# Layer 1 of a four-layer graph kernel: a constant in the cubic's real factor, and GpSimd's products merged and asked for earlier

## Chip, cores and metric

One core of one Trainium2 chip. The metric is the device time of one execution in microseconds (us), the median of several runs. In this text PE is TensorE, DVE is VectorE, ACT is ScalarE, POOL is GpSimd and SP is SyncE; PSUM is the matrix engine's accumulator memory and SBUF the on-chip working memory.

## What is computed

Four graph layers over 3327 nodes with 64 features, each `x = layernorm(x + layer(x, adj))`. The change lies in layer 1, whose core is, cut to what matters:

```python
left = x_tan @ att_W[:D] + att_b
right = x_tan @ att_W[D:]
adj_att = sigmoid(left + right.T) * adj            # N x N
x_local = _logmap(x[:, None, :], x[None, :, :], C) # N x N x D
support_t = einsum('ij,ijd->id', adj_att, x_local)
return _proj(_expmap(x, support_t, C), C)
```

The kernel never forms the N x N x D array. For every pair of nodes the scalar weight of `_logmap` is a function of one number, a scaled scalar product of the two rows, and the kernel uses a cubic in it, written as a real linear factor times (a square plus a constant). So per pair (i, j) it needs: a scalar product p, the attention product u = sigmoid(...) * adj, then a = (p + root term) * u, q = (scale * p + shift)^2, v = (q + constant) * a, and a matmul that sums v times the rows of j.

## The kernel before, in words

N is padded to 3328 = 26 blocks of 128. In the hyperbolic layer (`near_sphere`) a block of 128 nodes j lies on the partitions and nodes i lie along the free dimension. The work is 104 tiles of 128 x 832: two halves of i (`cp` 0 and 1), in each half all 26 blocks j, in each block two chunks of 2 x 416 columns. Two tiles with the same block are called a pair here; pair p has tiles 2p and 2p+1.

For each tile t:

- `products(t)`: PE, matmuls of `ljT` and `riT` into a PSUM tile `pq` (3 buffers, L1099).
- `attention(pair)`: the DMA of the block's adjacency rows `at` (4 buffers, L1057; four blocks are resident in `kept`), ACT's sigmoid of 128 x 1664 into `sg` (2 buffers, L1075), and then two POOL products `u = sg * at` of 128 x 832, one for each chunk (4 buffers, L1086).
- `linear(t)`: DVE's `a = (pq + dl) * u` (L1111), then ACT's square of `pq` in place (L1112). `dl` is one value per partition, so a different one for each j.
- `gather(t)`: DVE's `v = (pq + 1.757) * a` (L1120), PE's sum of `v` against the rows `xv` into `acc` (L1132), and `products(t + 3)`.
- `rows_of_sums`: in the first half only, ACT scales one block of `xv` (128 x 63, L1226) for each pair.

The order on PE, ACT, DVE and POOL is written out by hand (`manual_schedule`), so each engine's queue is exactly the order of the calls. In the loop, iteration t calls `linear(t + 1)`, then `gather(t)`, and when t is even `attention(t // 2 + 2)` and `rows_of_sums`. DVE's queue is thus a(1), v(0), a(2), v(1), ...; ACT's is, for each pair, sigmoid, `xv`, square, square.

Before the loop DVE makes `xf`, two columns and the rows `ri` (`rows_of_i`, L1218), POOL makes `dl` and `al` (L1255 to L1257), PE transposes the rows `lf`, `lj` and `ri`, and ACT and DVE copy these out of PSUM (L1210: `rows_j`, `rows_a` and `rows_b` on DVE, the others on ACT). After the loop `near_end` finishes the layer with small operations on 128 x 26 statistics; layers 2 and 3 follow.

Of the kernel before, what the change touches and what calls it, by code (L numbers as in the profile page):

```python
# [19 lines left out]
P = 128  # L20
# [40 lines left out]
CUBIC_ROOT = -1.39229596292  # L61
CUBIC_SHIFT = 0.0453813261445
CUBIC_REST = 1.75705840270866
NEIGH = 100
# [10 lines left out]
def kernel(  # L75
# [819 lines left out]
    with tc.tile_pool(name="l1", bufs=1) as l1:  # L895
# [20 lines left out]
        with tc.tile_pool(name="l1a", bufs=1) as l1a, tc.tile_pool(  # L916
# [86 lines left out]
            vec(ga, vq[:, 1], rq[:, 1], ALU.mult)  # L1003
            stt(inv_s, vq[:, 1], -0.5 / 0.9, r2[:, 1], op0=ALU.mult, op1=ALU.mult)
            sca(aa, g1, -1.0, 1.0, ALU.mult, ALU.add)
            vec(gas, ga, s, ALU.mult)
            stt(lj[:, :, D - 1], aa, 1.0, inv_s, op0=ALU.add, op1=ALU.mult)
        in_order.close()

        def near_sphere(mT, ljT_0, xm, sq_e, t_e, rows_63):  # L1010
# [3 lines left out]
            with tc.tile_pool(name="n1", bufs=1, reuse_waits="tile") as n1, tc.tile_pool(  # L1014
# [50 lines left out]
                def attention(pair):  # L1065

                    if pair >= len(tiles) // 2:
                        return
                    cp, jb, _ = tiles[2 * pair]
                    at, sl = load(cp, jb), slot(jb)  # L1070
                    sg = n1w.tile([P, 2, 2 * CW], F32, tag="sg", name=f"sg_{pair}")
                    lbs = lbh[:, :, cp * 2 * CW : (cp + 1) * 2 * CW]

                    def sigmoid(of):
                        nc.scalar.activation(  # L1075
                            sg[:, :, of], lbs[:, :, of], AF.Sigmoid, bias=rb[:, sl : sl + 1]
                        )

                    chunks = (slice(0, CW), slice(CW, 2 * CW))
                    if pair:  # L1080
                        sigmoid(slice(0, 2 * CW))
                    for ci, of in enumerate(chunks):
                        if not pair:
                            sigmoid(of)
                        u = n1w.tile(TW, F32, tag="u", bufs=4, name=f"u_{pair}_{ci}")
                        nc.gpsimd.tensor_tensor(u, sg[:, :, of], at[:, :, of], ALU.mult)  # L1086
                        us[2 * pair + ci] = u
                        yield
# [16 lines left out]
                def linear(t):  # L1105

                    if t >= len(tiles):
                        return
                    one = slice(slot(tiles[t][1]), slot(tiles[t][1]) + 1)
                    a_s[t] = n1w.tile(TW, F32, tag="a", bufs=3, name=f"a_{t}")  # L1110
                    stt(a_s[t], pqs[t], dl[:, one], us.pop(t), op0=ALU.add, op1=ALU.mult)  # L1111
                    nc.scalar.activation(  # L1112
                        pqs[t], pqs[t], AF.Square, bias=al[:, one], scale=gas[:, one]
                    )
# [109 lines left out]
                def rows_of_sums(jb):  # L1224
                    sl = slot(jb)
                    nc.scalar.activation(  # L1226
                        xv[:, sl, : D - 1], xc[:, sl, : D - 1], AF.Copy, scale=xf[:, sl : sl + 1]
                    )
# [12 lines left out]
                with tc.manual_schedule(  # L1241
# [6 lines left out]
                    keep((NB - 3, NB - 4))  # L1248
                    stt(xf, gas, CUBIC_LEAD / -256.0, gas, op0=ALU.mult, op1=ALU.mult)
                    nc.vector.tensor_copy(ri[:, :, D - 1], ga)  # L1250
                    vec(xv[:, :, D - 1], lj[:, :, D - 1], xf, ALU.mult)
                    rows_of_i(0, 4)
                    rows_of_i(4, NBH)

                    nc.gpsimd.tensor_scalar(dl, g1, CUBIC_ROOT, -1.0, ALU.mult, ALU.add)  # L1255
                    nc.gpsimd.tensor_tensor(dl, dl, inv_s, ALU.mult)
                    nc.gpsimd.tensor_scalar(al, ga, -1.0, CUBIC_SHIFT, ALU.mult, ALU.add)  # L1257
                    spread_a, spread_b = bank(0, left, 0, 4), bank(1, left, 13, 4)
# [6 lines left out]
                    spread_d = alone(left, 17, 3)  # L1265
                    rows_j(copy)
                    spread_c()
                    spread_d()
                    next(start)
                    rows_a = alone(turn, 0, 4)  # L1270
                    rows_a(copy)
                    changed = alone(wrong, 9, 4)
                    changed()
                    rows_b = alone(turn, 4, 4)
                    rows_b(copy)
                    first_ps.close()
                    n1q = pairs.enter_context(
# [9 lines left out]
                    linear(0)  # L1287
                    seventh()
                    for t in range(len(tiles)):
                        linear(t + 1)  # L1290
# [6 lines left out]
                        if t % 2 == 0:  # L1297
                            list(attention(t // 2 + 2))
                            if t // 2 + 2 < NB:
                                rows_of_sums(order[t // 2 + 2])  # L1300
                        if t == 8:
                            spread_left(7)
                        if t == len(tiles) - 4:
# [5 lines left out]
                            gp.tensor_tensor(gk, gs, ga, ALU.mult)  # L1309
                            gp.tensor_tensor(gss, gs, s, ALU.mult)  # L1310
                            gp.tensor_tensor(gks, gk, s, ALU.mult)
                            gp.tensor_scalar(gks, gks, -2.0, None, ALU.mult)
                            gp.tensor_tensor(gs2, gs, gs, ALU.mult)
# [10 lines left out]
                        if t == len(tiles) - 2:  # L1324
# [5 lines left out]
                                t_e.rearrange("p (a k h) -> p a k h", a=2, k=3), pm[..., P:]  # L1330
                            )
                    stt(rxn, r2[:, 0], -0.5, inv_s, op0=ALU.mult, op1=ALU.mult)
                    vec(xn, aa, rxn, ALU.mult)

        def near_end(mT, ljT, xm, sq_e, t_e, rows_63, x2):
# [4 lines left out]
            with tc.tile_pool(name="l1e", bufs=1) as l1e, tc.tile_pool(  # L1340
# [6 lines left out]
                def st(tag):  # L1347
                    return l1e.tile([P, NB], F32, name=f"e_{tag}")
# [70 lines left out]

                gt, q, k, ps = st("gt"), st("q"), st("k"), st("ps")  # L1420
                gp = st("gp")
# [42 lines left out]
                vec(k, p, gks, mul)  # L1464
                vec(gp, p, gss, mul)
                vec(k, k, gt, add)
                vec(ps, p, s, mul)

# [49 lines left out]
                vec(be, be, ck, sub)  # L1518
                alp = of(mul, al, ps, "alp")
                al2 = of(mul, al, al, "al2")  # L1520
# [39 lines left out]
                for b in (3, 1, 2):  # L1560
                    times(mw[b], mT, w_m, *fours[b])
                vec(be, be, s, mul)
                n_r = of(mul, var, t, "n_r")
                vec(n_r, n_r, t, mul)
                stt(n_r, n_r, -3.0, t, op0=add, op1=mul)
                alpha, beta = dl, xf
                stt(alpha, n_r, -0.5, al, op0=mul, op1=mul)
                stt(beta, n_r, -0.5, be, op0=mul, op1=mul)

                for b, g, n in ((0, 0, 1), (0, 1, 3), (3, 12, 1), (1, 4, 4), (2, 8, 4)):  # L1570
# [4 lines left out]
                    vec(lj[:, sl], lj[:, sl], one(beta, sl), mul)  # L1575
                    vec(lj[:, sl], lj[:, sl], pt, add)

                for g, n in threes:
                    sl = slots(g, n)
                    vec(x2[:, sl], x2[:, sl], one(alpha, sl), mul)  # L1580
                    vec(xc[:, sl], xc[:, sl], one(beta, sl), mul)
                    vec(x2[:, sl], x2[:, sl], xc[:, sl], add)
# [270 lines left out]
```

## Time and profile before

| | |
|---|---|
| median of 3 runs | 560.18 us (558.49 to 561.34) |
| the profiled execution | 559.12 us, of which 557.4 us is its span |
| first a (tile 0) starts | 22.22 us |
| last v (tile 103) ends | 226.66 + 1.02 = 227.68 us |
| busy over the span: PE, DVE, ACT, POOL | 525.1, 377.8, 276.2, 215.5 us |

All times in rows are microseconds from the start of the span, unless they are the mean of one instruction, which is in ns. A group's row gives the line of the code, engine and operation, output<-inputs, the shapes and a count, then the busy time and the mean of one, then the idle time of the engine just before these instructions and what ended it. In a timeline row the first number is the start and the second the duration of that row's instructions. Consecutive instructions of one engine overlap a little in these records[...]: DVE starts the instruction after a v 0.93 us later though a v has a duration of 1.02 us. The distance between two starts, not the duration, is what an engine spends on each.

### The profile page before, as it was taken

The page shows a single profiled execution, that of the slowest core. Times are in us where ns is not written, and L with a number is a line of the kernel's source. Part 1 is how long each engine was busy: PE and PEld are TensorE (multiplying, and loading weights), DVE is VectorE, ACT ScalarE, POOL GpSimd, SP SyncE. Part 2 cuts the span into 40 slices and gives each one's busy share as a digit, 9 for nine tenths or more (in the row PEclk, how much of TensorE's full clock was granted, in tenths as well). Part 3 has the DMA queues.
Part 4 walks back from the last instruction along what each step waited for, and adds up shares of the span by engine and source line. Part 5 has one row for each costly group of instructions (what it writes and reads, how often), then busy time and mean ns, then how long its engine had stood idle before and what let it go on. Part 6 is the DMA issues. An engine that isn't in the chain of part 4 may idle for free.

```text
span 557.4 us, 7490 instructions
## 1 busy us (share of the span) xinstructions
PE 525.1 (94%) x2841; PEld 226.5 (41%) x2841; DVE 377.8 (68%) x547; ACT 276.2 (50%) x323; POOL 215.5 (39%) x138
## 2 busy tenths in 40 slices
PE   7889989999999999999999999999999999999991
PEld 5522222222222222764444444444455555545541
DVE  6899999999999999899000010300578877887733
ACT  4799999999999998530000100000364333433321
POOL 3699999999999999300000000000001000000000
PEclk9899999999999999899999999999999999999996
DMA  8977776766676717799999039999019994799601
GB/s 287 357 254 232 209 229 201 224 210 227 206 237 211 220 60 272 294 427 425 422 423 418 16 141 422 420 426 413 15 55 328 342 327 177 244 270 362 257 1 37
DMA packets 33893, 143.57 MB, mean 258 GB/s; under 512 B 10269, under 2 KB 11959, under 8 KB 28855
## 3 DMA queue, kind: packets, MB, share of 16 engines
q1 hardware_dynamic: 31511, 142.40, 69.9%
q10 hardware_dynamic: 2336, 0.59, 0.5%
q8 instruction: 24, 0.39, 0.3%
q14 instruction: 22, 0.18, 0.1%
HBM read 141.53 MB, written 0.87 MB: 255 GB/s over the span
## 4 chain that ended last, share of the span: by engine, by line
PE 66%; DVE 20%; ACT 8%; issue 3%; DMA 1%; DVEq 0%
PE cnt L419 25%; PE pq L1099 12%; DVE v L1120 12%; PE cnt L524 11%; PE acc L720 6%; ACT sg L1075 4%; PE acc L735 3%; ACT pq L1112 3%; DVE a L1111 2%; DVE w L537 1%; PE cnt L410 1%; DVE mask L339 1%; DMA x<-in_x 1%; PE x_w L1435 1%; PE pn_l L371 1%
## 5 line engine op out<-in xcount | busy, mean ns | idle before, releaser
L1086 POOL TENSOR_TENSOR u<-sg,at 128x832 f32<-128x832 f32 x88 | 169.9, 1959 | 3.5 <-ACT sg L1075 3.1
L1099 PE MATMUL pq<-riT,ljT 64*128 64x416 f32 x416 | 100.2, 560 | 15.2 <-DVE v L1120 6.2
L1111 DVE SCALAR_TENSOR_TENSOR a<-pq,dl,u 128x832 f32<-128x832 f32 x104 | 112.1, 1078 | 2.9 <-PE pq L1099 2.8
L1112 ACT ACTIVATE pq<-pq,al,gas 128x832 f32<-128x832 f32 x104 | 105.0, 1011 | 15.2 <-DVE a L1111 14.3
L1120 DVE SCALAR_TENSOR_TENSOR v<-pq,a 128x832 f32<-128x832 f32 x104 | 105.8, 1017 | 1.1 <-ACT pq L1112 0.7
L1132 PE MATMUL acc<-v,xv 128*64 128x416 f32 x416 | 95.4, 537 | 0.1
L1075 ACT ACTIVATE sg<-lb,rb 128x1664 f32<-128x1664 f32 (+1 forms) x53 | 87.3, 1647 | 0.1
L539 ACT ACTIVATE w<-cnt 128x832 int16<-128x832 f32 x55 | 47.2, 863 | 71.5 <-PE cnt L524 71.4
L419 PE MATMUL cnt<-at_l,lj 128*64 128x416 f32 x448 | 80.2, 513 | 0.0
L651 POOL TENSOR_TENSOR s<-sq,s 128x384 bf16<-128x384 f32 (+1 forms) x4 | 4.1, 1026 | 195.0 <-ACT s L650 195.0
L504 ACT ACTIVATE x<-cnt 128x416 f32<-128x416 f32 x8 | 4.1, 517 | 130.6 <-PE cnt L419 130.6
L1099 PEld LDWEIGHTS pq<-riT,ljT 64*128 64x128 f32 x416 | 31.5, 184 | 88.3 <-DVE v L1120 83.0
L537 DVE TENSOR_SCALAR w<-cnt 128x832 int16<-128x832 f32 x49 | 50.2, 1024 | 25.2 <-PE cnt L524 23.8
L524 PE MATMUL cnt<-mask,tri 128*128 128x416 bf16 x208 | 53.5, 339 | 0.1
L720 PE MATMUL acc<-w,s 128*128 128x416 bf16 x208 | 52.6, 339 | 0.5 <-DVE hid L792 0.5
L524 PE MATMUL cnt<-mask,rest 128*128 128x416 bf16 x200 | 51.6, 340 | 1.2 <-ACT w L539 0.6
L419 PEld LDWEIGHTS cnt<-at_l,lj 128*64 128x64 f32 x448 | 31.9, 137 | 46.0 <-issue 45.2
L1132 PEld LDWEIGHTS acc<-v,xv 128*64 128x64 f32 x416 | 20.6, 134 | 61.0 <-issue 57.8
L339 DVE TENSOR_SCALAR mask<-ah 128x1664 bf16<-128x1664 f32 x42 | 43.4, 1034 | 0.5 <-DMA ah<-in_adjT 0.5
L407 DVE COPY lj<-pn_l 128x512 f32<-128x512 f32 (+1 forms) x4 | 2.4, 592 | 60.9 <-PE pn_l L371 60.9
L419 PE MATMUL cnt<-kept,lj 128*64 128x416 f32 x224 | 41.2, 513 | 0.0
L1086 POOL TENSOR_TENSOR u<-sg,kept 128x832 f32<-128x832 f32 x16 | 31.0, 1959 | 3.6 <-ACT sg L1075 3.6
(286 smaller groups left out, 411.7 us busy)
## 6 DMA issues: line engine op xcount, KB each, us to landing
at_l<-in_adjT SPq DMA_DIRECT2D x24, 1664.0 KB, 13.2
at<-in_adjT SPq DMA_DIRECT2D x44, 832.0 KB, 5.0
ah<-in_adjT SPq DMA_DIRECT2D x42, 832.0 KB, 6.5
bt_l<-in_adjT SPq DMA_DIRECT2D x8, 1664.0 KB, 16.8
kept<-in_adjT SPq DMA_DIRECT2D x7, 1664.0 KB, 9.2
lb<-lf_rows SPq DMA_DIRECT2D x2, 384.0 KB, 4.3
ljT<-ljT SPq DMA_DIRECT2D x4, 128.0 KB, 5.2
x<-in_x ACTq DMA_DIRECT2D x1, 416.0 KB, 5.3
```

Source lines behind the costliest of these rows:

```text
L339: nc.vector.tensor_scalar(mask[q], at, 0.0, None, ALU.not_equal)
L419: nc.tensor.matmul(acc[c][h * D : (h + 1) * D, :], hw[:, slot(jb), :], blocks[jb][:, o : o + CW], start=c not in begun, stop=last, skip_gr ...
L524: nc.tensor.matmul(cnt[c][:, e, :], mat, mask[q][:, of], start=start, stop=(mat is tri), skip_group_check=True,)
L537: nc.vector.tensor_scalar(w.bitcast(I16), cnt[c], 0.0, None, ALU.max)
L720: nc.tensor.matmul(acc[h, c][:, e, :], s12[:, slot(jb)].rearrange("p t d -> p (t d)"), ws[q, c][:, e, :], start=first, stop=last,)
L1075: nc.scalar.activation(sg[:, :, of], lbs[:, :, of], AF.Sigmoid, bias=rb[:, sl : sl + 1])
L1086: nc.gpsimd.tensor_tensor(u, sg[:, :, of], at[:, :, of], ALU.mult)
L1099: nc.tensor.matmul(pq[:, h, :], ljT[h != jb // NBH][rows, of], riT[rows, ch * CW : (ch + 1) * CW], start=True, stop=True,)
L1111: stt(a_s[t], pqs[t], dl[:, one], us.pop(t), op0=ALU.add, op1=ALU.mult)
L1112: nc.scalar.activation(pqs[t], pqs[t], AF.Square, bias=al[:, one], scale=gas[:, one])
L1120: stt(w, pqs.pop(t), CUBIC_REST, a_s.pop(t), op0=ALU.add, op1=ALU.mult)
L1132: nc.tensor.matmul(accs[cp, ci][h * D : (h + 1) * D, :], xv[:, slot(jb), :], w[:, h, :], start=(jb == orders[cp][0]), stop=(jb == orders[c ...
```

## The change

Five things.

1. The rows `lj` are scaled by `s` on DVE (`scaled`, three pieces) and the last columns hold other values, so that the linear factor's shift is the same for all j: a is now `(pq + CUBIC_PLUS) * u`, with a constant in place of the per-partition `dl`. The square takes `ga` in place of `gas`, `xv` is scaled by a new `gss = xf * s`, and a few small multiplications by `s` disappear or move in `near_end`.
2. The product is written over the sigmoid's tile: `u` disappears and `sg` gets 4 buffers.
3. From pair 2 on POOL makes both chunks of a pair in one instruction of 128 x 1664.
4. `attention` is called one pair further ahead (`t // 2 + 3`), with `attention(2)` before the loop.
5. POOL's first product stands behind a one-column copy, `after`, of the last piece that DVE scales; `rows_j` and `rows_a` are copied by ACT, and the second half of the first sigmoid is asked for after them.

```diff
+CUBIC_PLUS = 2 * CUBIC_ROOT - 1
...
-            stt(inv_s, vq[:, 1], -0.5 / 0.9, r2[:, 1], op0=ALU.mult, op1=ALU.mult)
...
-            stt(lj[:, :, D - 1], aa, 1.0, inv_s, op0=ALU.add, op1=ALU.mult)
+            sca(lj[:, :, D - 1], aa, 1.0, None, ALU.add)
...
-                    sg = n1w.tile([P, 2, 2 * CW], F32, tag="sg", name=f"sg_{pair}")
+                    sg = n1w.tile([P, 2, 2 * CW], F32, tag="sg", bufs=4, name=f"sg_{pair}")
...
-                    for ci, of in enumerate(chunks):
+                    wide = slice(0, 2 * CW)
+                    for of in chunks if pair < 2 else (wide,):
                         if not pair:
                             sigmoid(of)
-                        u = n1w.tile(TW, F32, tag="u", bufs=4, name=f"u_{pair}_{ci}")
-                        nc.gpsimd.tensor_tensor(u, sg[:, :, of], at[:, :, of], ALU.mult)
-                        us[2 * pair + ci] = u
+                        nc.gpsimd.tensor_tensor(sg[:, :, of], sg[:, :, of], at[:, :, of], ALU.mult)
+                        for ci, c in enumerate(chunks):
+                            if of in (c, wide):
+                                us[2 * pair + ci] = sg[:, :, c]
...
-                    stt(a_s[t], pqs[t], dl[:, one], us.pop(t), op0=ALU.add, op1=ALU.mult)
+                    stt(a_s[t], pqs[t], CUBIC_PLUS, us.pop(t), op0=ALU.add, op1=ALU.mult)
                     nc.scalar.activation(
-                        pqs[t], pqs[t], AF.Square, bias=al[:, one], scale=gas[:, one]
+                        pqs[t], pqs[t], AF.Square, bias=al[:, one], scale=ga[:, one]
                     )
...
-                    stt(xf, gas, CUBIC_LEAD / -256.0, gas, op0=ALU.mult, op1=ALU.mult)
-                    nc.vector.tensor_copy(ri[:, :, D - 1], ga)
+                    def scaled(b, n):
+
+                        sl = slice(2 * b, 2 * (b + n))
+                        vec(
+                            lj[:, sl, : D - 1], lj[:, sl, : D - 1],
+                            s[:, sl].unsqueeze(2).to_broadcast([P, 2 * n, D - 1]), ALU.mult,
+                        )
+
+                    scaled(9, 4)
+                    sca(ri[:, :, D - 1], ga, -CUBIC_ROOT, None, ALU.add)
+                    rows_of_i(0, 4)
+                    stt(xf, ga, CUBIC_LEAD / -256.0, ga, op0=ALU.mult, op1=ALU.mult)
                     vec(xv[:, :, D - 1], lj[:, :, D - 1], xf, ALU.mult)
-                    rows_of_i(0, 4)
-                    rows_of_i(4, NBH)
-
-                    nc.gpsimd.tensor_scalar(dl, g1, CUBIC_ROOT, -1.0, ALU.mult, ALU.add)
-                    nc.gpsimd.tensor_tensor(dl, dl, inv_s, ALU.mult)
-                    nc.gpsimd.tensor_scalar(al, ga, -1.0, CUBIC_SHIFT, ALU.mult, ALU.add)
+                    vec(gss, xf, s, ALU.mult)
+                    rows_of_i(4, 8)
+                    scaled(5, 4)
+                    rows_of_i(8, NBH)
+                    scaled(0, 5)
+
+                    nc.gpsimd.tensor_scalar(
+                        al, ga, CUBIC_PLUS, CUBIC_SHIFT - CUBIC_ROOT, ALU.mult, ALU.add
+                    )
+
+                    after = n1.tile([P, 1], F32, name="after")
+                    nc.gpsimd.tensor_copy(after, lj[:, 0, :1])
...
-                    rows_j(copy)
                     spread_c()
                     spread_d()
-                    next(start)
+                    rows_j()
                     rows_a = alone(turn, 0, 4)
-                    rows_a(copy)
+                    rows_a()
                     changed = alone(wrong, 9, 4)
                     changed()
                     rows_b = alone(turn, 4, 4)
                     rows_b(copy)
+                    next(start)
...
                     seventh()
+                    list(attention(2))
                     for t in range(len(tiles)):
...
-                            list(attention(t // 2 + 2))
+                            list(attention(t // 2 + 3))
...
-                vec(ps, p, s, mul)
...
-                vec(be, be, s, mul)
...
+                vec(beta_c, beta, s, mul)
```

More of the change, by code (lines that the diff above doesn't have):

```diff
@@ L1226, in rows_of_sums @@
                     nc.scalar.activation(
-                        xv[:, sl, : D - 1], xc[:, sl, : D - 1], AF.Copy, scale=xf[:, sl : sl + 1]
+                        xv[:, sl, : D - 1], xc[:, sl, : D - 1], AF.Copy, scale=gss[:, sl : sl + 1]
                     )
@@ L1309, in near_sphere @@
                             gp.tensor_tensor(gk, gs, ga, ALU.mult)
-                            gp.tensor_tensor(gss, gs, s, ALU.mult)
-                            gp.tensor_tensor(gks, gk, s, ALU.mult)
-                            gp.tensor_scalar(gks, gks, -2.0, None, ALU.mult)
+                            gp.tensor_scalar(gks, gk, -2.0, None, ALU.mult)
                             gp.tensor_tensor(gs2, gs, gs, ALU.mult)
@@ L1331, in near_sphere @@
                             )
+                    stt(inv_s, vq[:, 1], -0.5 / 0.9, r2[:, 1], op0=ALU.mult, op1=ALU.mult)
                     stt(rxn, r2[:, 0], -0.5, inv_s, op0=ALU.mult, op1=ALU.mult)
@@ L1418, in p_of @@
                         )
-                gt, q, k, ps = st("gt"), st("q"), st("k"), st("ps")
+                gt, q, k = st("gt"), st("q"), st("k")
                 gp = st("gp")
@@ L1464, in near_end @@
                 vec(k, p, gks, mul)
-                vec(gp, p, gss, mul)
+                vec(gp, p, gs, mul)
                 vec(k, k, gt, add)
-                vec(ps, p, s, mul)
                 first = in_bank("first_w")
@@ L1518, in near_end @@
                 vec(be, be, ck, sub)
-                alp = of(mul, al, ps, "alp")
+                alp = of(mul, al, p, "alp")
                 al2 = of(mul, al, al, "al2")
@@ L1565, in near_end @@
                 stt(n_r, n_r, -3.0, t, op0=add, op1=mul)
-                alpha, beta = dl, xf
+                alpha, beta, beta_c = dl, xf, gss
                 stt(alpha, n_r, -0.5, al, op0=mul, op1=mul)
@@ L1580, in near_end @@
                     vec(x2[:, sl], x2[:, sl], one(alpha, sl), mul)
-                    vec(xc[:, sl], xc[:, sl], one(beta, sl), mul)
+                    vec(xc[:, sl], xc[:, sl], one(beta_c, sl), mul)
                     vec(x2[:, sl], x2[:, sl], xc[:, sl], add)
```

## The prediction, made before the changed kernel was run

> **What bounds the kernel now.** I read the page first, then the timeline of layer 1, then the waits. The chain of waits gives layer 1's loop (a at 22.22 us to the last v's end at 227.68 us) to three engines in turn: v on DVE, pq on PE, the sigmoid on ACT. That is a loop with several nearly equal engines, so their distances between starts matter and not their shares. The groups on the page:
>
> ```profile
> L1086 POOL TENSOR_TENSOR u<-sg,at 128x832 f32<-128x832 f32 x88 | 169.9, 1959 | 3.5 <-ACT sg L1075 3.1
> L1111 DVE SCALAR_TENSOR_TENSOR a<-pq,dl,u 128x832 f32<-128x832 f32 x104 | 112.1, 1078 | 2.9 <-PE pq L1099 2.8
> L1112 ACT ACTIVATE pq<-pq,al,gas 128x832 f32<-128x832 f32 x104 | 105.0, 1011 | 15.2 <-DVE a L1111 14.3
> L1120 DVE SCALAR_TENSOR_TENSOR v<-pq,a 128x832 f32<-128x832 f32 x104 | 105.8, 1017 | 1.1 <-ACT pq L1112 0.7
> ```
>
> a and v have one shape, one PSUM input, one SBUF input and the same pair of operations; they differ in the scalar, a column of `dl` in a and a constant in v. The column costs 61 ns an instruction. DVE waits 4 us in all and POOL hardly: both are full. Which sets the pace? POOL's rows of the timeline:
>
> ```profile
> 84.79 46.55 POOL L1086 TENSOR_TENSOR u<-sg,at 128x832 f32<-128x832 f32 x24 [1.01 <-ACT sg L1075]
> 131.74 77.26 POOL L1086 TENSOR_TENSOR u<-sg,at 128x832 f32<-128x832 f32 x40 [0.41 <-ACT sg L1075]
> ```
>
> In the second half POOL runs 40 products without a gap at 77.26/40 = 1.93 us, 3.863 us a pair. DVE alone would need 0.99 (start of a to start of v) + 0.93 (v to a) = 1.92, 3.85 a pair. From tile 56 (a at 133.72) to tile 102 (222.57) the loop takes 88.85/23 = 3.863 us a pair: POOL's pace. In the first half it is 3.88 us (tile 36 at 94.59 to tile 48 at 117.88, 23.29/6), and the timeline tells why:
>
> ```profile
> 103.98 0.33 ACT L1226 ACTIVATE xv<-xc,xf 128x63 f32<-128x63 f32 x1
> 104.22 1.00 ACT L1112 ACTIVATE pq<-pq,al,gas 128x832 f32<-128x832 f32 x1
> 104.27 1.08 DVE L1111 SCALAR_TENSOR_TENSOR a<-pq,dl,u 128x832 f32<-128x832 f32 x1
> ...
> 105.26 1.02 DVE L1120 SCALAR_TENSOR_TENSOR v<-pq,a 128x832 f32<-128x832 f32 x1
> ...
> 105.38 1.02 ACT L1112 ACTIVATE pq<-pq,al,gas 128x832 f32<-128x832 f32 x1 [0.16 <-DVE a L1111]
> 106.20 1.08 DVE L1111 SCALAR_TENSOR_TENSOR a<-pq,dl,u 128x832 f32<-128x832 f32 x1
> 106.33 1.67 ACT L1075 ACTIVATE sg<-lb,rb 128x1664 f32<-128x1664 f32 x1
> ...
> 107.90 0.33 ACT L1226 ACTIVATE xv<-xc,xf 128x63 f32<-128x63 f32 x1
> 108.14 2.11 ACT L1112 ACTIVATE pq<-pq,al,gas 128x832 f32<-128x832 f32 x2
> ...
> 109.17 1.02 DVE L1120 SCALAR_TENSOR_TENSOR v<-pq,a 128x832 f32<-128x832 f32 x1
> ```
>
> A square waits for its a (105.35 -> 105.38); behind it stand sigmoid, `xv` and the next square, which ends at 109.14, and only then v starts (109.17, not 109.11). From the square's start to that v is 3.79 us. That is a ring through ACT and DVE, and it is longest in the first half, since only there `xv` (0.24 us) is in it.
>
> **Part by part.**
>
> *A constant in a.* a should cost what v costs: 0.93 us from start to start instead of 0.99, so DVE needs 4 x 0.9325 = 3.73 us a pair. Second half: 3.863 -> 3.73 if POOL lets it, 26 x 0.13 = 3.5 us. First half: I solve the ring. Let x be the distance from a(t+1) to v(t), T the pair's period. DVE: T = x + 3 intervals. ACT: T + x = a's duration + 0.03 + 3.79. Before: T = x + 2.85 and T + x = 4.90, so T = 3.875 (3.88 measured: the ring is right). After: T = x + 2.80 and T + x = 4.84, so T = 3.82. So the first half gains 0.06 a pair, not 0.12: from pair 3 on, 23 x 0.06 = 1.4 us.
>
> *Products of both chunks at once.* No 128x1664 row exists on POOL. From rows: 128x832 takes 1.957 us, and a small product
>
> ```profile
> L1309 POOL TENSOR_TENSOR gk<-gs,ga 128x26 f32<-128x26 f32 x1 | 0.2, 239 | 0.1
> ```
>
> gives a slope of (1957-239)/806 = 2.13 ns, so 239 + 1638 x 2.13 = 3.73 us, some 3.70 from start to start: just under DVE's 3.73. The dearest end is that nothing is saved, 2 x 1.93 = 3.86; the cheapest is the slope alone, 1664 x 2.13 = 3.55. I take 3.70, the fit through both rows. [...] Writing over the input is at no cost: the in-place `dl` product of 128x26 (L1256) takes 242 ns beside 239.
>
> [...] The row: all 104 a lie between 1073 and 1085 ns with POOL at work all the time. [...] I add nothing.
>
> *A pair further ahead, four `sg`.* Steadily at no cost: a sigmoid then waits for an a of four pairs earlier. At the start it costs, since ACT must make one more sigmoid (1.57 us) before the loop settles. SP's order is unchanged apart from that; an `at` still waits for POOL four pairs earlier, with 5.0 us to landing against over 11 us of cover.
>
> *The start.* DVE's work before the loop grows from 15.81 to 18.20 us by three scalings of 504, 504 and 630 columns[...] (the distance between starts of 128x512 products in `near_end` is 0.60 us): 0.60 + 0.60 + 0.73, and 0.1 each for some small ones; it ends near 20.2 us. POOL's first product starts then at about 20.4 us instead of 18.50. From there: four single products, 20.4 + 4 x 1.93 = 28.1; pair 2's merged product ends at 31.9 us, so a(4) starts at 31.9 instead of 29.86 (+2.0). ACT on its side takes over two copies (0.5 us each) and the extra sigmoid, 2.6 us, against 0.5 us that it now idles: +2.1 us. Before: a(6) at 33.70. After: ACT reaches the square of tile 4 near 34.1, v(4) at 35.1, a(6) at 36.0 (+2.3). I take +2.2. PE is not late: its transposes wait for `lj` and `ri` pieces that DVE has done before PE comes to them (16.4 and 18.0 us). `rows_b` stays on DVE at 21.0 us, and the first pq at 21.1.
>
> *Small operations.* In `near_end` the product with `s` at 233.67 us leaves a chain of dependent work: -0.1. The one at 240.38 stood in a wait for a reciprocal: nothing. `beta_c` comes after `lj` is done, beside PE's next layer. `inv_s` moves to 227.6 us, into a wait of DVE of 0.79 us for PE; if that cover went it would cost 0.1. Two POOL products fewer at 227 us are off the path. Two PE stalls of DVE (1.17 us before tile 16, 1.14 before tile 28) stay: they are v(14) and v(26), a pq and then a, whatever DVE's pace.
>
> *What is late next.* In the second half DVE itself, with POOL 0.03 us a pair behind it; PE needs 0.97 + 0.92 us a tile by durations, 1.8 from start to start. Layer 2 starts from the layer's end: its transfers wait for the last `acc` matmuls, so the gain is passed on whole.
>
> Sum against the profiled execution: 559.1 + 2.2 - 1.4 - 3.5 - 0.1 = **556.3 us**. The profiled execution lies 1.1 us below the median, so against the median this is 557.4. A measurement of this kernel can tell about 0.5%, 2.8 us, from no change; the forecast gain is just that.
>
> **The rivals.**
> *ACT does not hold the first half* (0.25): if a's earlier ends and sigmoids no longer tied to POOL let the ring run at DVE's 3.73 us, the first half gains another 23 x 0.09 = 2.1 us and part of the start is made up: 553.8. For it: ACT waits 14.3 us for a now, idle time that an engine at its limit would not have. Against it: the solved ring gives the measured 3.88.
> *The constant saves nothing* (0.08): if a's 61 ns came from reading `u` beside POOL's writing, DVE stays at 3.85 and the loop pays the start and gets 26 x 0.01 back: 561. Against it: v reads a tile just like u.
> *Slower: the merged product is dear* (0.07). POOL sets the end: 28.1 + 50 x P + 4.7 (last product to last v). That is 227.7, today's end, at P = 3.9 us; at 4.0 it is 232.8, 564 us. For it: no row of this size. Against it: two separate ones take 3.86, and only a long or in-place instruction with a price of its own would exceed that.
> *The start is dearer* (0.2): the scalings meet POOL's work on `rest` at 16.1 us and each other's waits, +3.5 us instead of 2.2: 557.6.
> Base case 0.40.
>
> **How the numbers follow.** Faster by over 0.5% (under 556.3 from the profiled time, 557.4 from the median): the ACT rival, and half or more of the base: 0.55. Same: the rest of the base, the dear start, most of the constant rival: 0.38. Slower: the merged product and a little of the constant rival: 0.07. Range 553.2 to 560.0: from below the ACT rival to the dear start with the median's 1.1 us on top; beyond it lie the slow product and the useless constant.
>
> **What would show it.** a's group at 1017 ns; 50 POOL rows of 128x1664 at 3.73 us; POOL's first product at 20.4 us; a(4) near 31.9 and a(6) near 36.0; 3.82 us a pair in the first half with v waiting for ACT, 3.73 in the second; the last v's end near 225. It would be wrong if a stayed at 1078, if the merged product exceeded 3.8 us, or if DVE showed waits for POOL in the second half.

## The result, and the profile after

| | before | after |
|---|---|---|
| median, us (11 runs each, side by side) | 559.12 | 557.58 |
| lowest and highest | 558.37 to 561.34 | 556.09 to 559.05 |
| ratio, 95% interval | | 0.9964 [0.9949, 0.9979] |
| the profiled execution, and its span | 559.12, 557.4 | 557.54, 555.7 |
| first a starts | 22.22 | 22.20 |
| a(6) starts | 33.70 | 35.34 |
| last v ends | 227.68 | 224.34 |
| a pair, first half (a 36 to a 48) | 3.882 | 3.823 |
| a pair, second half (a 56 to a 102) | 3.863 | 3.725 |
| last v's end to layer 2's first matmul | 15.33 | 16.78 |

The kernel is 0.36% faster, 1.5 us. The same groups of the page after the change; a row gives busy time and the mean of one in ns, then the idle time before:

```profile
L1088 POOL TENSOR_TENSOR sg<-sg,at 128x1664 f32<-128x1664 f32 x44 | 163.7, 3738 | 3.7 <-ACT sg L1076 2.2
...
L1116 ACT ACTIVATE pq<-pq,al,ga 128x832 f32<-128x832 f32 x104 | 104.6, 1012 | 12.1 <-DVE a L1115 12.0
L1115 DVE SCALAR_TENSOR_TENSOR a<-pq,sg 128x832 f32<-128x832 f32 x104 | 105.3, 1013 | 4.5 <-PE pq L1103 2.3
L1124 DVE SCALAR_TENSOR_TENSOR v<-pq,a 128x832 f32<-128x832 f32 x104 | 105.4, 1014 | 3.3 <-ACT pq L1116 2.2
```

a now costs what v costs, 1013 ns beside 1014. v's listed waits for ACT have grown from 0.7 to 2.2 us, most of it at the start: v(1) and v(2) wait 0.33 and 1.15 us there, before 0 and 0.59. Inside the first half, where DVE has become quick enough to find the square late, v's waits (tiles 8 to 51) sum to 1.1 us instead of 0.1, most of them too short to be listed. POOL's rows of the timeline (start, duration):

```profile
20.06 0.19 POOL L1277 COPY after<-lj 128x1 f32<-128x1 f32 x1 [4.48 <-DVE lj L1256]
20.21 15.06 POOL L1088 TENSOR_TENSOR sg<-sg,kept 128x832 f32<-128x832 f32 x6
...
100.96 7.46 POOL L1088 TENSOR_TENSOR sg<-sg,at 128x1664 f32<-128x1664 f32 x2 [0.19 <-ACT sg L1076]
...
131.88 70.75 POOL L1088 TENSOR_TENSOR sg<-sg,at 128x1664 f32<-128x1664 f32 x19 [0.52 <-ACT sg L1076]
```

POOL starts later than before (20.21 instead of 18.50 us), pauses every second pair in the first half for ACT's sigmoid, and runs 19 merged products in the second half at 70.75/19 = 3.724 us. The ring of the first half, ACT's and DVE's rows:

```profile
104.86 1.01 DVE L1115 SCALAR_TENSOR_TENSOR a<-pq,sg 128x832 f32<-128x832 f32 x1
...
109.70 1.02 DVE L1124 SCALAR_TENSOR_TENSOR v<-pq,a 128x832 f32<-128x832 f32 x1
```

```profile
105.91 1.02 ACT L1116 ACTIVATE pq<-pq,al,ga 128x832 f32<-128x832 f32 x1 [0.16 <-DVE a L1115]
106.86 1.67 ACT L1076 ACTIVATE sg<-lb,rb 128x1664 f32<-128x1664 f32 x1
108.43 0.33 ACT L1230 ACTIVATE xv<-xc,gss 128x63 f32<-128x63 f32 x1
108.67 1.99 ACT L1116 ACTIVATE pq<-pq,al,ga 128x832 f32<-128x832 f32 x2
```

From the square at 105.91 to the v (109.70) that waits for the square behind sigmoid and `xv` it is 3.79 us as before, and from a to that v 4.84 us: the two numbers that the prediction's ring gave.

**Where the time went.** Stretch by stretch, the profiled executions differ by +1.64 us up to a(6), by -4.98 us from there to the last v's end (193.98 before, 189.00 after), by +1.45 us from there to layer 2, and by +0.19 us after that: -1.70 us of span. The +1.45 is not in the loop, and the diff's edits in that stretch only take out or move small multiplications. In the stretch from 229.2 to 236.2 us (columns: length, then busy time of PE, its weight load, DVE, ACT and POOL, the granted clock of PE, DMA) the first execution of this kernel has

```profile
229.20:236.20 7.00, 7.00 (x35) 7.00 (x35) 4.80 (x39) 4.72 (x13) 0.00 (x0) 0.52 0.99 421
```

about half the clock: PE is always busy but has 35 matmuls there. A second profiled execution of the same kernel (below) has 48 there, at clock 1.00, in 5.50 us of work.

### The profile page after: what moved, and what is told of

It reads as the page before. It is cut to its first block, busy times and chain, and to the rows that moved or that the text cites. A ratio compares the mean times of both kernels' runs of the same rounds, so it can differ in the third digit from the quotient of the medians.

```text
span 555.7 us, 7392 instructions
## 1 busy us (share of the span) xinstructions
PE 527.5 (95%) x2841; PEld 226.9 (41%) x2841; DVE 372.2 (67%) x549; ACT 276.8 (50%) x325; POOL 207.4 (37%) x85
## 4 chain that ended last, share of the span: by engine, by line
PE 68%; DVE 17%; issue 7%; ACT 6%; POOL 1%; DVEq 0%; POOLq 0%; ACTq 0%
PE cnt L421 26%; PE cnt L526 11%; DVE v L1124 10%; PE pq L1103 9%; PE acc L722 6%; PE acc L1136 4%; PE acc L737 3%; ACT pq L1116 3%; ACT sg L1076 2%; DVE a L1115 2%; DVE w L539 1%; PE cnt L412 1%; DVE mask L341 1%; PE idle L928 1%; PE x_w L1455 1%
## 5 line engine op out<-in xcount | busy, mean ns | idle before, releaser
L1088 POOL TENSOR_TENSOR sg<-sg,at 128x1664 f32<-128x1664 f32 x44 | 163.7, 3738 | 3.7 <-ACT sg L1076 2.2
L1116 ACT ACTIVATE pq<-pq,al,ga 128x832 f32<-128x832 f32 x104 | 104.6, 1012 | 12.1 <-DVE a L1115 12.0
L1115 DVE SCALAR_TENSOR_TENSOR a<-pq,sg 128x832 f32<-128x832 f32 x104 | 105.3, 1013 | 4.5 <-PE pq L1103 2.3
L421 PEld LDWEIGHTS cnt<-at_l,lj 128*64 128x64 f32 x448 | 31.9, 137 | 46.2 <-issue 45.4
L586 DVE TENSOR_TENSOR x<-x,xc 128x416 f32<-128x416 f32 x4 | 2.4, 588 | 41.5 <-ACT x L506 41.5
```

What stands on the lines that cost most here:

```text
L421: nc.tensor.matmul(acc[c][h * D : (h + 1) * D, :], hw[:, slot(jb), :], blocks[jb][:, o : o + CW], start=c not in begun, stop=last, skip_gr ...
L1088: nc.gpsimd.tensor_tensor(sg[:, :, of], sg[:, :, of], at[:, :, of], ALU.mult)
L1115: stt(a_s[t], pqs[t], CUBIC_PLUS, us.pop(t), op0=ALU.add, op1=ALU.mult)
L1116: nc.scalar.activation(pqs[t], pqs[t], AF.Square, bias=al[:, one], scale=ga[:, one])
```

## The experiments

Periods of a pair in the loop's two halves, starts of a(6) and ends of the last v, and ratios to the kernel before with their intervals:

| kernel | first half, second half | a(6), last v ends | ratio |
|---|---|---|---|
| before | 3.882, 3.863 | 33.70, 227.68 | |
| after | 3.823, 3.725 | 35.34, 224.34 | 0.9964 [0.9949, 0.9979] |
| column given back | 3.882, 3.846 | 35.49, 228.83 | 1.0039 [1.0023, 1.0056] |
| two products again | 3.820, 3.725 | 37.37, 226.26 | 0.9946 [0.9927, 0.9965] |
| before, constant only | 3.840, 3.838 | 32.47, 224.72 | 0.9958 [0.9947, 0.9969] |
| before, sigmoid a square earlier | 3.845, 3.847 | 34.39, 226.78 | 0.9988 [0.9979, 0.9998] |
| no gate | 3.822, 3.725 | 35.26, 224.28 | 0.9963 [0.9951, 0.9975] |
| xv behind the next square | 3.725, 3.725 | 35.49, 222.27 | 0.9919 [0.9899, 0.9938] |
| the same, no gate | 3.725, 3.725 | 35.18, 221.98 | 0.9925 [0.9905, 0.9946] |
| xv behind, two products | 3.725, 3.765 | 35.14, 222.92 | 0.9955 [0.9942, 0.9968] |
| xv behind, sigmoids later | 3.725, 3.725 | 35.69, 222.48 | 0.9913 [0.9889, 0.9936] |
| the same, no gate | 3.725, 3.725 | 37.22, 224.02 | 0.9937 [0.9913, 0.9962] |
| two pairs ahead | 4.68 in the second half | | one execution: 599.95 us |

**The changed kernel again, a second profiled execution.** No edit.

> The changed kernel once more, unedited, for a second look at the granted clock after the loop. If the 6.8 us at half clock there (229.2 to 235.9 us) is a matter of when a spell falls and not of the change: another length or none, and from the last v's end to the next layer's first matmul about 15.35 us instead of 16.78. If the change itself brings it about: 6.8 us and 16.8 again.

The loop is the same to 0.01 us a pair (3.822 and 3.725, last v's end 224.29). From there to layer 2 it takes 15.37 us instead of 16.78, and the execution 555.96 us instead of 557.54:

```profile
229.20:236.20 7.00, 5.50 (x48) 5.30 (x48) 5.37 (x43) 5.08 (x14) 0.00 (x0) 1.00 1.01 426
```

So the 1.4 us behind the loop belong to the execution and not to the change. Spells at half the clock, 3.4 or 6.8 us long, stand in each of the twelve traces for which the clock was taken in steps of 0.5 us, besides one at the end of the span in before and after, in whose last 11.1 us PE is idle (mean clock 0.57 and 0.59): before has one from 12.0 to 18.9 us and one from 233.9 to 237.3, after has 14.1 to 17.5, 27.8 to 31.2 and 229.2 to 236.0. The ten of them that cover the end of layer 1 bear the reading out: from the last v's end to layer 2 it takes 15.33 to 15.38 us in the five that have no spell there, 15.33 to 15.71 in the four with one of 3.4 us, and 16.78 in the one with 6.8 us.

In the 3.4 us ahead of the spell of 6.8 us PE is recorded as busy throughout (3.40 of 3.40 us from 225.8 to 229.2), at clock 1.00 up to 229.0; what brings this spell about is not shown.

Of the other ten timed runs of the kernel only the mean clock is known. Of all eleven, the two at 0.987, the second execution's clock, took 556.1 and 556.3 us, and the nine at 0.979 to 0.983 took 557.3 to 559.1. That fits one spell more in most runs than in the second execution; where it fell is not known, and the kernel before shows no such plain order.

**The column given back.** What the constant is worth, all else as changed:

```diff
-                    stt(a_s[t], pqs[t], CUBIC_PLUS, us.pop(t), op0=ALU.add, op1=ALU.mult)
+                    stt(a_s[t], pqs[t], plus, us.pop(t), op0=ALU.add, op1=ALU.mult)
```

`plus` is a 128 x 1 tile that POOL fills with CUBIC_PLUS.

> The changed kernel with one edit: a takes the same number from a one-column tile instead of an instruction constant. If the constant is what shortens a: a's mean goes back from 1013 to about 1077 ns, the second half runs at DVE's 3.85 us a pair instead of 3.72 (26 x 0.13 = 3.3 us) and the first half at the ring's 3.875 instead of 3.82 (23 x 0.055 = 1.3 us); the last v ends near 229.0 instead of 224.3 us and the time is about 4.6 us above the changed kernel's, near 562. If the gain came from GpSimd's merged and earlier products alone: no change, 557.6.

```profile
L1115 DVE SCALAR_TENSOR_TENSOR a<-pq,plus,sg 128x832 f32<-128x832 f32 x104 | 111.6, 1073 | 4.4 <-PE pq L1103 2.3
```

The same value, once read from a column and once a constant, makes 1073 or 1013 ns: the 60 ns are the column's. The second half then takes 3.846 us a pair, twice 0.99 + 0.93: DVE's own pace with a column, and not the 3.863 of before. The last v ends 4.5 us later than in the changed kernel, and the time is above the kernel before.

**Two products again**, with the rest of the change (lead, four `sg`, constant):

```diff
-                    for of in chunks if pair < 2 else (wide,):
+                    for of in chunks:
```

> The changed kernel with two products of 128x832 for each pair, in place, instead of one of 128x1664. If the merged product is what frees the second half (as the prediction had it, 3.863 us a pair on POOL against 3.73): the second half goes back to 3.863 and the last v ends near 227.8, time near 561. If what mattered is that POOL no longer waits for sigmoids (four buffers, a pair further ahead): POOL runs without a gap from 20.2 us, 104 x 1.93 = 200.9, so it ends at 221.1 and the last v near 224.3, because its lead of some 3 us at half time is just used up at the end; time near 557.7, with a(4) some 1.5 us earlier than with the merged product.

```profile
36.89 49.94 POOL L1088 TENSOR_TENSOR sg<-sg,at 128x832 f32<-128x832 f32 x26
87.61 119.16 POOL L1088 TENSOR_TENSOR sg<-sg,at 128x832 f32<-128x832 f32 x62 [0.79 <-DVE v L1124]
```

The second half stays at 3.725 us although POOL needs 2 x 119.16/62 = 3.84 us a pair. POOL hardly stops, in the first half too, where DVE needs 3.82 and loses another 2.3 us at two stalls for PE; with a longer lead it has by then a stock of products that it uses up. At a(56) the product is ready 3.8 us ahead of its a, at a(100) still 1.2 us. That a(6) stands at 37.37 goes with a spell of half clock from 15.1 to 22.0 us ahead of it, in which PE's transposes are late (first a at 23.71); the edit changes nothing ahead of a(4). The whole loop (first a to last v's end) takes 202.55 us instead of 202.14, but the difference lies ahead of a(6): from there it is 188.89 us instead of 189.00. So in the changed kernel the merged product buys nothing in the settled loop, and not the 3.5 us that the second half gained; in the times, 0.9946 and 0.9964, the two do not stand apart either.

**The kernel before with the constant alone.** All j get the same linear factor, another one than the layer needs; the instructions are those of the kernel before.

```diff
-                    stt(a_s[t], pqs[t], dl[:, one], us.pop(t), op0=ALU.add, op1=ALU.mult)
+                    stt(a_s[t], pqs[t], CUBIC_ROOT, us.pop(t), op0=ALU.add, op1=ALU.mult)
```

> The kernel before with one edit: a takes a constant instead of its column (the linear factor is then another one than the layer needs). If the loop is bound by POOL and by ACT's ring as read: a falls to 1014 ns, yet the second half stays at 3.863 us a pair and the first half goes from 3.88 to 3.86 at best, so the last v ends at 226.9 to 227.7 and the time is within 1 us of before's. If DVE alone were the bound: 104 x 0.06 = 6.3 us less, the last v near 221.4.

```profile
129.41 76.79 POOL L1086 TENSOR_TENSOR u<-sg,at 128x832 f32<-128x832 f32 x40 [0.39 <-ACT sg L1075]
```

The second half does not stay at 3.863 but falls to 3.838, and POOL makes 40 products in 76.79 instead of 77.26 us, with nothing changed on POOL. Either the column slows POOL's products, or 3.863 was never POOL's pace. The rows of the kernel before show what else it can be, DVE's, ACT's and POOL's in turn:

```profile
151.11 1.08 DVE L1111 SCALAR_TENSOR_TENSOR a<-pq,dl,u 128x832 f32<-128x832 f32 x1
...
156.90 1.08 DVE L1111 SCALAR_TENSOR_TENSOR a<-pq,dl,u 128x832 f32<-128x832 f32 x1
```

```profile
152.22 1.02 ACT L1112 ACTIVATE pq<-pq,al,gas 128x832 f32<-128x832 f32 x1 [0.35 <-DVE a L1111]
153.16 1.67 ACT L1075 ACTIVATE sg<-lb,rb 128x1664 f32<-128x1664 f32 x1
```

```profile
154.91 1.96 POOL L1086 TENSOR_TENSOR u<-sg,at 128x832 f32<-128x832 f32 x1
```

a(t+1) ends at 152.19, its square starts at 152.22, the sigmoid behind it at 153.16, the product at 154.91, and a(t+4) when that ends: 5.79 us, and 1.93 more to a(t+5), where the next round begins. That is 7.72 us for two pairs, 3.86 each: a second ring, of four steps on three engines (a on DVE, square and sigmoid on ACT, product on POOL). In it POOL has only gaps of some hundredths of a microsecond, too small for the profile to call them waits: over pairs 30 to 49 its starts lie 1.91 us apart inside a pair, and 1.95 us from one pair to the next.

**The kernel before with the sigmoid a square earlier** tells the two apart, with the column kept:

```diff
+                    list(attention(2))
                     for t in range(len(tiles)):
...
                         if t % 2 == 0:
-                            list(attention(t // 2 + 2))
                             if t // 2 + 2 < NB:
                                 rows_of_sums(order[t // 2 + 2])
+                        else:
+                            list(attention((t + 1) // 2 + 2))
```

> The kernel before (column, single products, two sg), with nothing changed but the call of attention: for each pair it stands one tile earlier, so ACT's sigmoid comes ahead of the second square of a pair instead of behind it. In the kernel before, the second half's rows close a ring: a (151.11 us) - its square (152.22) - the sigmoid (153.16) - POOL's product (154.91) - the a three tiles later (156.90), 5.79 us for three tiles, 3.86 a pair. Theory A, that ring set the second half's 3.863: with the sigmoid a square earlier it falls to DVE's own 3.846 (as in the kernel with the column given back), POOL's free pace of 2 x 1.92 = 3.84 being just below; first half also to about 3.85, since sigmoid and xv no longer stand together; second half's 46 tiles 0.4 us shorter. Theory B, POOL's own pace set it, because the column read slows its product: the second half stays at 3.863 with POOL without a gap at 1.93. The start may cost up to 2 us, since a sigmoid more stands ahead of the loop; time within 0.5% of the kernel before by both.

```profile
129.50 76.85 POOL L1086 TENSOR_TENSOR u<-sg,at 128x832 f32<-128x832 f32 x40 [0.38 <-ACT sg L1075]
```

Both halves fall to 3.846 us, DVE's pace with a column, and POOL makes 40 products in 76.85 us beside a DVE that reads the column. POOL's starts now lie 1.91 us apart inside a pair and 1.92 to the next. So the ring set the second half, and POOL's own pace is 1.92 us, 3.84 a pair. What this kernel gains in the loop it pays in part at the start (a(6) 34.39 instead of 33.70).

**xv behind the next square.** If ACT's ring holds the first half, taking `xv` out of it must bring DVE's pace there:

```diff
                             list(attention(t // 2 + 3))
-                            if t // 2 + 2 < NB:
-                                rows_of_sums(order[t // 2 + 2])
+                        elif t // 2 + 2 < NB:
+                            rows_of_sums(order[t // 2 + 2])
```

> The changed kernel with ACT's scaling of a block of xv asked for after odd tiles instead of after even ones, so that it stands behind the next square and not ahead of it. If ACT's ring (square, sigmoid, xv, square, v) sets the first half: the ring loses 0.24 us, falls below DVE's 3.72 us a pair, the first half goes from 3.82 to 3.73 (23 x 0.09 = 2.1 us), no v waits for a square there, and the last v ends near 222.2; time near 555.5. If ACT's sum of work set it (3.7 us a pair of issue) or POOL did: 3.82 stays and 557.6.

```profile
103.02 1.01 ACT L1116 ACTIVATE pq<-pq,al,ga 128x832 f32<-128x832 f32 x1
103.95 0.34 ACT L1230 ACTIVATE xv<-xc,gss 128x63 f32<-128x63 f32 x1
104.23 1.02 ACT L1116 ACTIVATE pq<-pq,al,ga 128x832 f32<-128x832 f32 x1
105.18 1.67 ACT L1076 ACTIVATE sg<-lb,rb 128x1664 f32<-128x1664 f32 x1
106.75 1.01 ACT L1116 ACTIVATE pq<-pq,al,ga 128x832 f32<-128x832 f32 x1
```

It does: 3.725 us in both halves. `xv` now fills a wait of the square for its a (the next square starts 0.28 us after it, where it had to wait anyway), and between the square at 104.23 and the next at 106.75 only the sigmoid stands. The last v ends 2.1 us earlier than in the changed kernel; with 554.61 us, a ratio of 0.9919, the kernel is faster than both.

**The same with two products.** With POOL's stock no longer refilled in a slower first half, the merged product should count:

```diff
-                    for of in chunks if pair < 2 else (wide,):
+                    for of in chunks:
```

> xv asked for after odd tiles, and two products of 128x832 for each pair. With the ring short, DVE could run at 3.725 us a pair throughout; two products take POOL 2 x 1.92 = 3.84. If the merged product is worth something only when ACT's ring no longer hides POOL: 104 x 1.92 = 199.7 us from POOL's first product near 20.3 puts its end at 220.0 and the last v near 223.2, 1 us later than with the merged product (222.3) but with no 3.725 kept up in the second half; time near 555.5. If the merged product is worth its 0.115 us a pair over all 50 pairs: 5.8 us, time near 560.

```profile
210.09 3.93 POOL L1088 TENSOR_TENSOR sg<-sg,kept 128x832 f32<-128x832 f32 x2
```

```profile
210.22 1.02 DVE L1115 SCALAR_TENSOR_TENSOR a<-pq,sg 128x832 f32<-128x832 f32 x1
...
214.05 1.02 DVE L1115 SCALAR_TENSOR_TENSOR a<-pq,sg 128x832 f32<-128x832 f32 x1
```

It does, but only near the end. POOL makes 88 products in 168.80 us without a stop, 3.84 a pair, and DVE at 3.725 catches up with it by 0.1 us a pair: the product is ready 2.0 us ahead of a(40), 0.35 ahead of a(80), and from a(86) on each pair's first a starts as its product ends (214.02 and 214.05 in the rows), 3.83 us a pair. The average of the second half is 3.765. From a(6) to the last v's end it takes 187.78 us instead of 186.79 with merged products, so there the merged product is worth 1.0 us; it gives 0.35 of that back at the start, where a(6) comes later with it (35.49 instead of 35.14).

**No gate.** The copy `after` and its tile are left out, so POOL's first product needs only its sigmoid.

> The changed kernel without the one-column copy that holds POOL's first product back until DVE has scaled its last piece. My theory: the gate is most of what the new start costs. POOL then begins near 17.5 us, its second product near 21.2 (it waits for ACT), pair 2's merged product ends near 30.7 instead of 31.6 us, and a(4) follows[...]. Loop from a(0) to the last v's end shorter by some 0.8 us or a(0) earlier; time 0.5 to 1 us below the changed kernel's. Rival: [...] a(0) and a(4) are later than with the gate: time 1 to 2 us above.

DVE's rows ahead of the loop:

```profile
17.90 2.46 DVE L1256 TENSOR_TENSOR lj<-lj,s 128x504 f32<-128x504 f32 x1
20.28 0.80 DVE L1222 SCALAR_TENSOR_TENSOR mT<-xc,gas 128x630 f32<-128x630 f32 x1
```

POOL's first product starts at 17.59 us, and the scaling that DVE asks for next takes 2.46 us instead of 0.68: it ends at 17.90 + 2.46 = 20.36 us, 0.54 us after POOL's product (17.59 + 2.23 = 19.82). Beside that product, this one piece with two SBUF inputs cost 1.78 us more. Against the expectation a(4) does not come at 30.7 but at 31.54 us (31.61 with the gate), and a(6) is 35.26 instead of 35.34: the gate neither costs nor saves, since v(1) and v(2) wait for ACT's squares in both (0.88 and 1.16 us without it). Together with `xv` behind the next square it changes nothing either (last v's end 221.98 instead of 222.27, times 554.88 and 554.61):

> xv asked for after odd tiles and no gate, together. If both hold by themselves, they add, because with a short ring DVE follows POOL from the start: 3.73 us a pair throughout, last v near 221.4 us, time 0.5 to 1 us below that with xv alone (554.6). If the gate is needed, above it.

**Sigmoids later at the start.** On the kernel with `xv` behind the next square, ACT's sigmoids of pairs 2 and 3 go behind the squares of tiles 1 and 2:

```diff
-                    list(attention(2))
                     for t in range(len(tiles)):
                         linear(t + 1)
                         if t == 0:
                             by_rows()
                             rows_of_sums(order[1])
+                            list(attention(2))
+                        if t == 1:
+                            list(attention(3))
...
                         if t % 2 == 0:
-                            list(attention(t // 2 + 3))
+                            if t:
+                                list(attention(t // 2 + 3))
```

> The changed kernel with xv behind the next square, and with ACT's sigmoids of pairs 2 and 3 asked for one square later each (behind the squares of tiles 1 and 2 instead of ahead of them). Theory A, ACT alone holds the start: v(1) and v(2) no longer wait for squares, a(4) starts near 30.7 us instead of 31.6, a(6) near 34.5 and the last v ends near 221.4 us. Theory B, POOL holds it just as much, since its first product stands behind the gate at 20.2 us: four single products and a merged one end at 20.2 + 4 x 1.93 + 3.70 = 31.6 us, so a(4) stays at 31.6, a(6) at 35.3, the last v's end at 222.2 us and the time at 0.992 of the kernel before. I expect B.

```profile
29.05 1.02 DVE L1124 SCALAR_TENSOR_TENSOR v<-pq,a 128x832 f32<-128x832 f32 x1 [0.21 <-ACT pq L1116]
31.96 1.02 DVE L1115 SCALAR_TENSOR_TENSOR a<-pq,sg 128x832 f32<-128x832 f32 x1 [1.88 <-POOL sg L1088]
```

In the changed kernel these two read

```profile
30.48 1.02 DVE L1124 SCALAR_TENSOR_TENSOR v<-pq,a 128x832 f32<-128x832 f32 x1 [1.15 <-ACT pq L1116]
31.61 1.02 DVE L1115 SCALAR_TENSOR_TENSOR a<-pq,sg 128x832 f32<-128x832 f32 x1
```

The wait for ACT is nearly gone, and a(4) waits for POOL instead and starts no earlier. Both engines were due at the same time: ACT with its extra sigmoid, and POOL, which started at 20.21 us and finished its first merged product near 31.6.

**And without the gate as well**, the one kernel in which the start should gain:

> As the kernel with later sigmoids, and POOL's first product is not held behind DVE's last scaling either. If ACT and POOL hold the start together, only this one gains: POOL's second product starts near 21.4 us (as without the gate before), so pair 2 ends at 21.4 + 3 x 1.93 + 3.70 = 30.9 us: a(4) 30.9 instead of 31.6, last v's end 221.5 us, time 0.991. If the gate or the sigmoids alone hold it, this is either at 222.2 like the others (something third holds it), or no better than the one with later sigmoids alone.

```profile
17.65 1.92 DVE L1266 TENSOR_TENSOR gss<-xf,s 128x26 f32<-128x26 f32 x1
```

It did not, but for a reason beside the question: a small product of 128 x 26, 0.18 us elsewhere, now took 1.92 us and ended at 19.57 us, 0.04 us after POOL's first product (17.54 + 1.99 = 19.53), PE's transposes were late (first a at 23.73) with a spell of half clock from 15.2 to 22.0 us, as in the kernel with two products, and POOL's second product started at 23.53 us instead of 21.4, when its sigmoid was there. Whether the start gains when both holds are gone is not settled.

**The changed kernel with attention two pairs ahead**, as in the kernel before:

```diff
-                    list(attention(2))
...
-                            list(attention(t // 2 + 3))
+                            list(attention(t // 2 + 2))
```

> The changed kernel with attention asked for two pairs ahead as in the kernel before, all else left (merged products, constant, gate). Theory A, the merged product needs the longer lead: the sigmoid of pair p+2 is asked for at v(2p), and a(2p+4) then waits for sigmoid 1.6 + square ahead of it 1.0 + merged product 3.7 us = 6.3 us or more, while DVE's four instructions until that a take only some 2.8 + 0.9 = 3.7 us: T of some 5 us a pair or more, 52 x 1.3 us = 60 us or more longer, over 610 us. Theory B, the lead is only a cushion: loop longer by less than 3 us, 558 to 561 us.

```profile
L1088 POOL TENSOR_TENSOR sg<-sg,at 128x1664 f32<-128x1664 f32 x44 | 163.6, 3719 | 43.8 <-ACT sg L1076 43.8
```

40 us slower than the kernel before, though less than expected: POOL waits 43.8 us for sigmoids. It is the ring of a, square, sigmoid and product again, with a product of 3.73 us in it: without the column's 0.06 its three tiles take about 5.73 - 1.92 + 3.73 = 7.5 us, with one more tile (1.87) 9.4 for two pairs, 4.7 each; 4.68 is measured. So the merged product needs the longer lead.

## Why the prediction was right, and where it was not

The time of 557.58 us lies in the range, 1.3 us above the forecast of 556.3; the gain stays under the 0.5% that the prediction held for just likelier than not. That 557.4, the forecast against the median, was met almost exactly is luck: it added 1.1 us because three runs of the kernel before had a median of 560.18, and over eleven the median is 559.12, that of the profiled execution itself.

- **The constant**: right. 1017 ns were forecast for a, 1013 measured; giving the column back undoes it alone.
- **The first half**: right. The solved ring gave 3.82 us a pair, measured 3.823; taking `xv` out of it gives DVE's 3.725. The rival in which ACT does not hold the first half is out.
- **The second half**: the size is right (3.73 forecast, 3.725 measured), the reason wrong. The step that failed reads "That is POOL's pace" of the 77.26/40 = 1.93 us, and from it followed that the merged product frees the loop. The 3.863 were a ring through a, square, sigmoid and product: a sigmoid one square earlier brings 3.846 with single products and with the column. POOL's own 3.84 a pair, reached with the constant alone (3.838), would have been the next limit, and the longer lead gets round that: with two products it stays at 3.725 for as long as the loop lasts. The merged product has the forecast cost, 3738 ns where the fit gave 3.73 us (from 1957 ns for a single product, which in the rows is 1959), but is worth nothing here once the loop has settled. Writing over the sigmoid's tile costs nothing, as forecast: single products take 1.92 us each in place and 1.92 into a tile of their own. The row without a gap misled: POOL's gaps were too short to be listed.
- **The start**: +2.2 forecast, +1.6 at a(6). POOL's first product came at 20.21 (20.4 forecast), a(4) at 31.61 (31.9), a(6) at 35.34 (36.0): the terms were each a little too large. Both holds that the prediction named are there, and taking either away alone moves nothing; the copies that ACT took over were given back in no run. Against the kernel with the constant alone, whose front has a half-clock spell of the same 3.4 us, the start costs 2.9 us (32.47). So part of what the kernel before lost there was probably its own longer spell, but that rests on one execution of each.
- **From a(6) to the last v's end**: -4.9 forecast (-1.4 and -3.5), -4.98 measured.
- **Behind the loop**: -0.1 forecast, +1.45 in the profiled execution and +0.04 in the second. "The gain is passed on whole" holds for the second execution alone, which at 555.96 us is 0.3 from the forecast of 556.3.

Of the rivals, the useless constant is out by the returned column, the dear merged product by its 3738 ns, the dear start by a(6). What the prediction had no case for is that 1.5 us can come and go with the place of PE's half-clock spells, as much as the whole measured gain. The median's distance from the forecast is about that; the other runs' mean clocks fit a spell more in most of them, but since they have no trace, that the spell explains it is argued, not shown.

The constant alone on the kernel before gives 0.9958, as much as the whole change. It leaves out the scaling of the rows that a true constant needs, so this is no cheaper way to the same result. In the profiled executions its last v's end, 224.72, is 3.0 us ahead of before's: 1.7 us won from a(6) on, and 1.2 ahead of a(6), where before had the longer spell. Everything else in the change moves the last v's end by another 0.4 us, 3.3 won from a(6) on and 2.9 lost at the start.

## What to carry to other kernels

An engine without listed gaps is not yet the bound: work out its own pace from a stretch in which nothing can hold it, and if that is quicker than the loop, be it by the 0.6% seen here (1.92 and 1.93 us), look for a ring through the engines that closes on it. In a loop of nearly equal engines, ask for the slow step one piece of work earlier, and take small work out of the place between two steps that a ring needs; here the move of one 0.24 us instruction gained as much again as the whole change. Before explaining a microsecond of a layer's end, look at the granted clock there, in more than one execution.

## What was not expected of the hardware

- A scalar that DVE reads from a 128 x 1 column costs 60 ns an instruction of 128 x 832 over a constant of the same value (1073 and 1013 ns, 104 instructions each).
- In each of the three kernels without the gate, a DVE product with two SBUF inputs that started 0.11 to 0.31 us after POOL's first product ended 0.04 to 0.67 us after that product did. It took 2.46 us instead of 0.68 for 128 x 504, 2.58 instead of 0.80 for 128 x 630 (the kernel with `xv` behind the next square) and 1.92 instead of 0.18 for 128 x 26. The 104 a and 104 v, with one SBUF input, took 1.01 to 1.03 us each in the same traces.
- PE's clock was halved for 6.8 us with PE recorded as busy all the time (7.00 of 7.00 us at a mean clock of 0.52, 35 matmuls instead of 48). PE was as busy in the 3.4 us ahead of it (3.40 of 3.40 us), and from 40 to 224 us the mean clock had been 1.00. In a second execution of the same kernel the clock was 1.00 in that stretch, with PE busy for 5.50 of the 7.00 us.
